# A post-norm decoder block: four products in column quarters, the bias product added to the residual, the last group's squares summed by products, and new places for every step

## The chip, the cores and the metric

The kernel runs on one core of a Trainium2 chip. TensorE (PE in the profile, PEld for its weight loads) multiplies, VectorE (DVE) and ScalarE (ACT) empty PSUM and do element work, GpSimd (POOL) does element work in SBUF alone, and SyncE (SP) issues nearly all DMAs. The metric is the device time of one execution in microseconds (us); less is better.

## What is computed

x is 128 sequences of 64 tokens by 128 features, and there is a context of the same shape. One decoder layer with a layer norm (LN) after each of its three parts:

```python
q, k, v = x@Wq+bq, x@Wk+bk, x@Wv+bv                  # 16 heads of 64
qp, kp = exp(q @ wq_feat), exp(k @ wk_feat)          # 32 features a head
x1 = LN(x + concat(qp @ (kp.T @ v) / (qp @ kp.sum(tokens) + 1e-6)) @ Wproj + bproj)
Q, K, V = x1@cWq.T+cbq, ctx@cWk.T+cbk, ctx@cWv.T+cbv # 16 heads of 8
x2 = LN(x1 + concat(softmax(Q @ K.T / sqrt(8)) @ V) @ Wo.T + bo)
h  = layernorm(gelu(x2 @ tern(W_fc).T), ln_w, ln_b)  # 512 hidden
out = LN(x2 + h @ tern(W_proj).T)
```

`tern` turns a weight into -1, 0 or 1. All of it is float32. The kernel folds weights together first: Wq and wq_feat, Wv and Wproj (the tile U), the biases (WB), the inner layer norm's weight and mean (w2c).

## The kernel before

The 8192 token rows are cut into 16 groups of 512 (8 sequences). For each group, `load`, `attn`, `cross` and `ffn` define short steps, each with a name: K0 to K3 and Q0 to Q3 are the feature products, ks and kT sum the keys, G is kp.T by x, D and dT make the denominators, E multiplies qp by their inverse, M is G by U, Y is qp by M and the residual, Yn the norm. Then xk, xq and xv make the cross attention's K, Q and V, X the scores for the row maxima, xm sends the maxima, S the scores again with exp, P the product with V, C the normalization, O the output product, xn the norm. ft, fb, fw, fs, fo, fv, fx and fn are the feed-forward part and the last norm; fn also stores the group.

Nothing is scheduled by the compiler. Each step has a place, `g * ROUND + SHIFT + PLACE` (ROUND is 44; a step of the weights' preparation has its place in PREP), and the program is the list of steps sorted by place (line 929). All engines take their instructions in that order. A group's steps spread over more than three rounds, so each round of the steady state holds attention of group g, cross attention of g-1 and g, and feed-forward of g-2 and g-3; cross and ffn steps are keyed by r = g + 1. Loads stand a round early.

PSUM has two pools: `one`, four tiles of 128x512, and `two`, two tiles of 128x1024. A step that asks for a tile waits until an earlier tile of that pool was read for the last time. fo0 and fo1 keep a `one` tile each until fx has read it.

A product of float32 is two MATMUL and two LDWEIGHTS instructions in the trace; one of fp32r operands (K, Q, E, fw, xk, xq, G) is one of each. A product is issued in one of several forms: with all 128x128 of the array (`128*128` in the trace), in four column quarters (`128*32`: four products, each with 32 columns of weights and 32 PSUM partitions, tile_position (0, 32j); M, Y, D, P and ks do this), or in row halves or 64x64 pieces (G, X, S).

Lines that the change touches: 596 is M's product, 610 Y's first product (dT by WB) and 615 its other products, 617 the sum with the residual xg; 635 the six copies of a product's pieces into krep or qrep by DMA, 659 xv's product, 712 the four DMAs of the row maxima, 771 O's product, 816 fs's square on ACT, 819 and 822 the sums of squares on POOL (line 410 in the trace), 833 fo's product and 834 the product that sums the squares over the hidden units.

```python
ps = z.fps[k] = one()
for i in range(2):
    n = slice((2 * k + i) * P, (2 * k + i) * P + P)
    o = 256 * i
    for c in range(NFC):
        nc.tensor.matmul(ps[:, o : o + WF], lhsT=z.gf[c // 2][:, c % 2, n], rhs=w.w2c[:, c, :], start=(c == 0), stop=(c == NFC - 1))
    nc.tensor.matmul(ps[:, o + WF : o + WF + 1], lhsT=z.sq[:, n], rhs=rff, start=True, stop=True)
```

Of the kernel before, what the change touches and what calls it, by code (L numbers as in the profile page):

```python
# [55 lines left out]
)  # L56
BIG = 5
# [27 lines left out]
def decoder_block(  # L85
# [347 lines left out]
    def shift(g, place):  # L433
        return SHIFT[2 if place[0] == "f" else 1 if place[0] in "xXSPCO" else 0].get(g, 0)
# [47 lines left out]
    def attn(g):  # L482
# [118 lines left out]

        @each(g, [f"Y{t}" for t in range(GT)])
        def _(t):
            if t == 0:
                z.x1 = later.l2.tile([P, GT, D], FP, tag="x1", name="x1")
                z.mv1 = st.tile([P, GT, 2], FP, tag="mv1", name="mv1")
            yps = one()
            for i in range(4):
                n = slice(t * P + 32 * i, t * P + 32 * i + 32)
                nc.tensor.matmul(yps[32 * i : 32 * i + 32, 0:D], lhsT=z.dT[:, n].bitcast(FP), rhs=w.WB.bitcast(FP), start=True,  # L610
                                 stop=False, tile_position=(0, 32 * i))
            for c in range(NC1):
                for i in range(4):
                    q = 2 * t + i // 2
                    nc.tensor.matmul(yps[32 * i : 32 * i + 32, 0:D], lhsT=z.qp[:, c, t * P + 32 * i : t * P + 32 * i + 32],  # L615
                                     rhs=z.m[q // 4][:, q % 4, c, :], start=False, stop=(c == NC1 - 1), tile_position=(0, 32 * i))
            nc.vector.tensor_tensor(z.x1[:, t, :], yps[:, 0:D], z.xg[:, t, :], ALU.add)
            stats(z.mv1, t, z.x1[:, t, :])
            if t == GT - 1:
                z.rs1 = rstd_of(z.mv1)  # L620
# [5 lines left out]
    def pieces(step, ps, bias, roles, rep):  # L626

        pc = later.t2.tile([P, 3, GN], BF, tag="pc", name="pc")
        nc.scalar.activation(pc[:, 0, :], ps, AF.Identity, bias=bias)
        r = later.t2.tile([P, GN], FP, tag="tmp", name="pr")  # L630
        nc.vector.scalar_tensor_tensor(r, ps, bias, pc[:, 0, :], ALU.add, ALU.subtract)
        copy(f"{step}1", pc[:, 1, :], r)
        tt(f"{step}2", pc[:, 2, :], r, pc[:, 1, :], ALU.subtract)
        for i, part in enumerate(roles):
            nc.sync.dma_start(out=rep[i::HD], in_=pc[:, part, :])

    def cross(g):
# [18 lines left out]
        def _():  # L656
            ps = one()
            for t in range(GT):
                nc.tensor.matmul(ps[:, t * P : t * P + P], lhsT=z.cT[:, t * P : t * P + P],
                                 rhs=w.cwvT.rearrange("p o c h e -> p (o c h e)"), start=True, stop=True)  # L660
# [42 lines left out]
        def _():  # L703
# [5 lines left out]
            for i in range(2):  # L709
                for h in range(2):  # L710
                    o = 64 * h + R2 - 2 + i
                    nc.sync.dma_start(out=qrep[o : o + 1], in_=mn[32 * h : 32 * h + 32, i, :])
# [52 lines left out]
        def _(k):  # L765
# [4 lines left out]
            for i in range(2):  # L770
                nc.tensor.matmul(ps[:, i * D : i * D + D], lhsT=z.cnT[k][:, i, :], rhs=w.cwo, start=True, stop=True)
# [11 lines left out]
    def ffn(g):  # L783
# [30 lines left out]
        def _(k):  # L814
            s = later.f1.tile([P, 2, GN], FP, tag="sk", name="sk")
            nc.scalar.activation(s.rearrange("p i n -> p (i n)"), z.gf[k].rearrange("p i n -> p (i n)"), AF.Square)  # L816
            if k == 0:
# [8 lines left out]
        @each(r, ("fo0", "fo1"))  # L826
        def _(k):
            ps = z.fps[k] = one()
            for i in range(2):
                n = slice((2 * k + i) * P, (2 * k + i) * P + P)  # L830
                o = 256 * i
                for c in range(NFC):
                    nc.tensor.matmul(ps[:, o : o + WF], lhsT=z.gf[c // 2][:, c % 2, n], rhs=w.w2c[:, c, :], start=(c == 0), stop=(c == NFC - 1))  # L833
                nc.tensor.matmul(ps[:, o + WF : o + WF + 1], lhsT=z.sq[:, n], rhs=rff, start=True, stop=True)  # L834
# [87 lines left out]
    groups = [SimpleNamespace(pt={}, kp={}, khl={}, cps={}, cnT={}, mps={}, gT={}, m={}, gf={}, fps={}) for _ in range(NG)]  # L922
# [52 lines left out]
```

## Time and profile before

| | |
|---|---|
| time, median of 3 runs | 740.73 us (740.13 to 741.4) |
| the profiled execution | 740.87 us, its span 738.9 us |
| mean granted TensorE clock | 0.966 |
| busy | PE 687.4, PEld 576.9, DVE 572.9, ACT 504.3, POOL 323.4 us |
| one steady round (374.68 to 415.36) | 40.68 us; PE 40.31, DVE 34.99, ACT 31.31, POOL 18.79 us busy |
| first 60 us | PE 49.4 us busy |
| from 660 us to the end (78.9 us) | PE 47.9 us busy |
| instruction DMA, queue q8 | 129 packets, 2.11 MB |

The span is from the first to the last instruction. A row of the timeline has the start in us, the length in us, the engine, the line, the operation, the tile written and the tiles read, the shape and the count of merged instructions; in brackets stands the idle time before it and what ended it. The lengths of matmuls overlap, so the cost of a product is read from the start of one row to the start of the next. In a row of the windows stand the stretch, its length, each engine's busy time, the granted clock of TensorE (1.00 is full), and the DMA engines' share and rate.

### The profile page before, as it was taken

The numbers are of one execution on the slowest core, as the hardware profiler recorded it, in microseconds if no ns is written. First come the engines' busy times: TensorE is split into PE (matmuls) and PEld (weight loads), VectorE is DVE, ScalarE is ACT, GpSimd is POOL, SyncE is SP. The second block draws the span as 40 slices with busy tenths as digits, with TensorE's granted clock in tenths as the row PEclk, the third lists the DMA queues.
The fourth block names the chain that finished last, engine by engine and source line by source line (L and its number), as shares of the span: only waits on it lengthen the run. The fifth ranks groups of instructions, "written<-read, shape, count | busy, mean of one in ns | idle before, by whom it ended". The sixth has DMA issues, their size and how long they took to land.

```text
span 738.9 us, 36655 instructions
## 1 busy us (share of the span) xinstructions
PE 687.4 (93%) x16551; PEld 576.9 (78%) x16551; DVE 572.9 (78%) x1379; ACT 504.3 (68%) x757; POOL 323.4 (44%) x383
## 2 busy tenths in 40 slices
PE   6989999999999999999999999999999999976753
PEld 5767878787878888887878788887888787865653
DVE  1568898797879797988879787979889796958532
ACT  2636565867688687877686886878686877654750
POOL 4744414263553626263634526262635445143451
PEclk9989999999999999999999999999999999996875
DMA  7005131302122131413032221314131312203000
GB/s 191 3 31 136 43 106 31 102 24 77 55 75 75 49 101 34 117 34 92 31 84 65 76 75 47 103 34 116 35 80 42 82 53 52 71 24 82 19 23 20
DMA packets 58428, 47.82 MB, mean 65 GB/s; under 512 B 7952, under 2 KB 54032, under 8 KB 58272
## 3 DMA queue, kind: packets, MB, share of 16 engines
q1 hardware_dynamic: 57632, 45.37, 22.6%
q8 instruction: 129, 2.11, 1.2%
q0 software_dynamic: 320, 0.08, 0.2%
q14 instruction: 27, 0.22, 0.1%
q10 hardware_dynamic: 320, 0.03, 0.0%
HBM read 15.58 MB, written 4.19 MB: 27 GB/s over the span
## 4 chain that ended last, share of the span: by engine, by line
PE 68%; DVE 18%; POOL 4%; ACT 4%; DMA 2%; issue 2%; SPq 1%; POOLq 0%; ACTq 0%; DVEq 0%
PE two L596 13%; PE one L833 8%; PE one L615 8%; PE one L427 6%; PE one L428 4%; PE one L429 4%; PE two L530 3%; DVE bns L390 3%; PE two L697 3%; POOL rstd L385 2%; PE one L517 2%; DVE x L851 2%; PE one L610 2%; DVE gT L395 2%; PE one L582 2%
## 5 line engine op out<-in xcount | busy, mean ns | idle before, releaser
L596 PE MATMUL two<-U,gT 128*32 128x128 f32 x4096 | 123.4, 275 | 0.8 <-DVE mx L700 0.5
L596 PEld LDWEIGHTS two<-U,gT 128*32 128x32 f32 x4096 | 112.0, 111 | 1.8 <-DVE mx L700 0.6
L397 ACT COPY m<-two 128x1024 f32<-128x1024 f32 x64 | 64.9, 1013 | 30.3 <-PE two L596 30.1
L399 POOL TENSOR_SCALAR khl<-kp 128x512 fp32r<-128x512 f32 x32 | 20.2, 631 | 137.6 <-ACT kp L496 137.6
L833 PE MATMUL one<-w2c,gf 128*128 128x130 f32 x512 | 78.1, 301 | 1.5 <-ACT gf L810 1.5
L700 DVE TENSOR_REDUCE mx<-two 128x16 f32<-128x1024 f32 x64 | 74.9, 1213 | 3.3 <-PE two L697 3.3
L833 PEld LDWEIGHTS one<-w2c,gf 128*128 128x128 f32 x512 | 71.4, 210 | 4.8 <-ACT gf L810 2.1
L410 POOL TENSOR_TENSOR sq<-sk 128x512 f32<-128x512 f32 x16 | 20.8, 1299 | 116.9 <-ACT sk L816 116.9
L385 POOL TENSOR_TENSOR rstd<-veps,mhalf 128x4 f32<-128x4 f32 x64 | 66.0, 1032 | 5.3
L615 PE MATMUL one<-m,qp 128*32 128x128 f32 x2048 | 68.1, 273 | 0.0
L383 POOL TENSOR_SCALAR veps<-mv 128x4 f32<-128x4 f32 x64 | 15.4, 240 | 116.2 <-DVE mv L844 73.8
L423 ACT ACTIVATE x<-x,nm,rstd 128x128 f32<-128x128 f32 x128 | 51.3, 482 | 20.6 <-DVE nm L422 20.6
L728 ACT ACTIVATE pt<-two 128x1024 f32<-128x1024 f32 x64 | 62.7, 1021 | 1.9 <-PE two L725 1.7
L390 DVE BATCH_NORM_STATS2 bns<-x 128x6 f32<-128x128 f32 x192 | 55.5, 289 | 5.5
L615 PEld LDWEIGHTS one<-m,qp 128*32 128x32 f32 x2048 | 57.4, 110 | 0.2 <-issue 0.2
L508 ACT ACTIVATE qp<-one,bqk 128x512 f32<-128x512 f32 x64 | 43.7, 684 | 16.3 <-PE one L429 12.0
L496 ACT ACTIVATE kp<-one 128x512 f32<-128x512 f32 x64 | 38.3, 598 | 22.0 <-PE one L429 13.5
L530 PE MATMUL two<-khl,xgh 64*128 64x512 f32 x256 | 49.0, 418 | 4.6 <-DVE gT L395 4.3
L707 ACT ACTIVATE mn<-one 64x128 bf16<-64x128 f32 x16 | 4.3, 270 | 70.1 <-PE one L705 70.1
L744 PE MATMUL one<-pt,vbd 128*32 128x64 f32 x2048 | 46.7, 224 | 0.5 <-DVE x L851 0.5
L410 POOL TENSOR_TENSOR sq<-sq,sk 128x512 f32<-128x512 f32 x32 | 40.9, 1280 | 6.1 <-ACT sk L816 4.8
L842 DVE COPY mv<-one 128x2 f32<-128x2 f32 x32 | 4.9, 154 | 49.4 <-PE one L834 49.4
(217 smaller groups left out, 1812.6 us busy)
## 6 DMA issues: line engine op xcount, KB each, us to landing
krep<-pc SPq DMA_DIRECT2D x96, 128.0 KB, 2.4
qrep<-pc SPq DMA_DIRECT2D x96, 128.0 KB, 3.0
xT<-in_x_T_dram SPq DMA_DIRECT2D x16, 256.0 KB, 3.1
xg<-in_x_dram SPq DMA_DIRECT2D x16, 256.0 KB, 3.1
cT<-in_ctx_T_dram SPq DMA_DIRECT2D x16, 256.0 KB, 3.3
out_dram<-x SPq DMA_DIRECT2D x16, 256.0 KB, 2.4
qrep<-mn SPq DMA_DIRECT2D x64, 8.0 KB, 1.8
wTk<-in_L_attn_Wk_T_dram SPq DMA_DIRECT2D x1, 512.0 KB, 4.4
```

Source lines behind the costliest of these rows:

```text
L385: nc.gpsimd.tensor_tensor(r, v, mhalf, ALU.pow)
L390: nc.vector.bn_stats(s, src)
L397: nc.scalar.copy(dst, src)
L410: eng.tensor_tensor(dst, a, b, op)
L423: nc.scalar.activation(x[:, t, :], x[:, t, :], AF.Identity, scale=r[:, t : t + 1], bias=nm[:, t : t + 1])
L530: nc.tensor.matmul(gps[:, b, :], lhsT=xp[r, t, :], rhs=z.khl[t // 2][r, kp, t % 2, :], start=(i == 0), stop=(i == 2), tile_position=(64 * ...
L596: nc.tensor.matmul(z.mps[b // 2][32 * j : 32 * j + 32, b % 2, c * D : c * D + D], lhsT=z.gT[b // 4][:, b % 4, h * F : h * F + F], rhs=w.U[ ...
L615: nc.tensor.matmul(yps[32 * i : 32 * i + 32, 0:D], lhsT=z.qp[:, c, t * P + 32 * i : t * P + 32 * i + 32], rhs=z.m[q // 4][:, q % 4, c, :], ...
L700: nc.vector.tensor_reduce(z.mx[:, :, :, t], sps.rearrange("p h (c k) -> p h c k", k=S), AX.X, ALU.max)
L728: nc.scalar.activation(z.pt[t].rearrange("p h b c q -> p (h b c q)"), sps.rearrange("p h n -> p (h n)"), AF.Exp, scale=HD ** -0.5)
L744: nc.tensor.matmul(z.cps[i // 4][32 * c : 32 * c + 32].rearrange("p (n k q) -> p n k q", k=2, q=32)[:, q // 32 : q // 32 + 2, k, :], lhsT= ...
L833: nc.tensor.matmul(ps[:, o : o + WF], lhsT=z.gf[c // 2][:, c % 2, n], rhs=w.w2c[:, c, :], start=(c == 0), stop=(c == NFC - 1))
```

## The change

The same sums are computed, in other forms and another order.

1. Products in column quarters: xv, O, and fo with its sum of squares. Each product with 128 columns of weights becomes four with 32.
2. A new step W makes dT by WB for the whole group, four full fp32r products, and adds it to xg; Y's own quarter products for this are gone (before, they read the same fp32r tiles as float32).
3. In the last group the POOL sums of squares are gone: fo multiplies the four squared tiles themselves with the column 1/512, accumulating in PSUM, and the second square has a buffer of its own.
4. `pieces` issues its six DMAs sorted by part, not by row; xm's four DMAs of 32x128 become two of 64x128.
5. All places are new, and EDGE adds a further shift to single steps of groups -1, 0, 1, 14, 15 and 16.

```diff
 def shift(g, place):
-    return SHIFT[2 if place[0] == "f" else 1 if place[0] in "xXSPCO" else 0].get(g, 0)
+    return SHIFT[2 if place[0] == "f" else 1 if place[0] in "xXSPCO" else 0].get(g, 0) + EDGE.get(g, {}).get(place, 0)
...
+        @at(g, "W")
+        def _():
+            ps = one()
+            for t in range(GT):
+                n = slice(t * P, t * P + P)
+                nc.tensor.matmul(ps[:, n], lhsT=z.dT[:, n], rhs=w.WB, start=True, stop=True)
+            nc.vector.tensor_tensor(z.xg.rearrange("p t d -> p (t d)"), ps, z.xg.rearrange("p t d -> p (t d)"), ALU.add)
...
-            for i in range(4):
-                n = slice(t * P + 32 * i, t * P + 32 * i + 32)
-                nc.tensor.matmul(yps[32 * i : 32 * i + 32, 0:D], lhsT=z.dT[:, n].bitcast(FP), rhs=w.WB.bitcast(FP), start=True,
-                                 stop=False, tile_position=(0, 32 * i))
...
-        for i, part in enumerate(roles):
+        for part, i in sorted((part, i) for i, part in enumerate(roles)):
             nc.sync.dma_start(out=rep[i::HD], in_=pc[:, part, :])
...
             for t in range(GT):
-                nc.tensor.matmul(ps[:, t * P : t * P + P], lhsT=z.cT[:, t * P : t * P + P],
-                                 rhs=w.cwvT.rearrange("p o c h e -> p (o c h e)"), start=True, stop=True)
+                for j in range(4):
+                    r = slice(32 * j, 32 * j + 32)
+                    nc.tensor.matmul(ps[r, t * P : t * P + P], lhsT=z.cT[:, t * P : t * P + P][:, r],
+                                     rhs=w.cwvT.rearrange("p o c h e -> p (o c h e)"), start=True, stop=True,
+                                     tile_position=(0, 32 * j))
...
             for i in range(2):
-                for h in range(2):
-                    o = 64 * h + R2 - 2 + i
-                    nc.sync.dma_start(out=qrep[o : o + 1], in_=mn[32 * h : 32 * h + 32, i, :])
+                nc.sync.dma_start(out=qrep[R2 - 2 + i :: R2], in_=mn[:, i, :])
...
-            s = later.f1.tile([P, 2, GN], FP, tag="sk", name="sk")
+            s = later.f1.tile([P, 2, GN], FP, tag="sk1" if k and g == NG - 1 else "sk", name="sk")
             nc.scalar.activation(s.rearrange("p i n -> p (i n)"), z.gf[k].rearrange("p i n -> p (i n)"), AF.Square)
-            if k == 0:
+            if g == NG - 1:
+                z.sk[k] = s
+            elif k == 0:
...
                 for c in range(NFC):
-                    nc.tensor.matmul(ps[:, o : o + WF], lhsT=z.gf[c // 2][:, c % 2, n], rhs=w.w2c[:, c, :], start=(c == 0), stop=(c == NFC - 1))
-                nc.tensor.matmul(ps[:, o + WF : o + WF + 1], lhsT=z.sq[:, n], rhs=rff, start=True, stop=True)
+                    for j in range(4):
+                        q = slice(32 * j, 32 * j + 32)
+                        nc.tensor.matmul(ps[q, o : o + WF], lhsT=z.gf[c // 2][:, c % 2, n][:, q], rhs=w.w2c[:, c, :],
+                                         start=(c == 0), stop=(c == NFC - 1), tile_position=(0, 32 * j))
+                for j in range(4):
+                    q = slice(32 * j, 32 * j + 32)
+                    sq = [z.sk[c // 2][:, c % 2, n] for c in range(NFC)] if g == NG - 1 else [z.sq[:, n]]
+                    for c, s in enumerate(sq):
+                        nc.tensor.matmul(ps[q, o + WF : o + WF + 1], lhsT=s[:, q], rhs=rff, start=(c == 0),
+                                         stop=(c == len(sq) - 1), tile_position=(0, 32 * j))
```

O is changed as xv is. The new places are a table; sorted by them, a steady round (the seventh, counted from 0 the sixth) reads as follows, with g left out:

```
before: P0 P1 S2 P2 P3 S3 fx xk G0 G1 D0 D1 P4 D3 P6 C0 xt G2 G3 K0 xq fw0 D2 M0 dT P5 M1 P7 fs0 M4 M5 M2 M3 C1 fw1 O0
        K1 E2 E1 xv X0 X1 K2 lc lx E0 ks0 xs ks1 M6 M7 E3 K3 lgs O1 X2 X3 fs1 Y0 ks2 Y2 Y1 ks3 Y3 xm Q0 Q1 fn xn fo0 Q3 lg
        kT xr S0 S1 Q2 Yn fo1 fv ft lxs fb
after:  xs Q0 ft Q2 S0 S1 fo1 Q3 Q1 Yn S3 lg fb fv P0 P1 P2 P3 fx S2 xk G0 G1 D0 lxs D2 D1 D3 P4 C0 xt G2 G3 dT xq fw0
        P6 M0 P5 P7 M1 M4 M5 E2 E1 fw1 C1 xr E3 E0 K0 K1 M2 M3 O0 fs0 lx ks0 xv X0 X1 W K2 K3 lc X2 ks1 ks2 Y0 M6 fs1 X3 O1
        lgs M7 Y2 xm fn xn ks3 Y1 fo0 Y3 kT
```

In the last rounds the order is looser. After the last group's Y3 before come 15.xm, 13.fo0, 15.S0, 15.S1, 15.Yn, 13.fo1, 13.fv, 14.ft, and only after 15.P0 to 15.S3 16.xk, 13.fx, 16.xt, 16.xq; after the change come 15.S0, 13.fo1, 13.fv, 13.fx, 15.S2, 15.Yn, 15.P0, 15.P1, 15.S1, 15.S3, 16.xk, 14.ft, 16.xt, 16.xq. (The number is the round's key: 16.xq is the last group's.) At the very end 15.fo1 moves ahead of 16.xn, 15.fo0 between 16.ft and 16.fw0, and 15.fx behind 16.fo0. In the first round the fill of krep and qrep (x2) moves from behind M5 of group 0 to behind its ks1, the bias tiles (wb) from behind D3 to behind Q0, and x is loaded straight after the key weights. The store of group 0 (its fn) moves into the round of group 14.

More of the change, by code (lines that the diff above doesn't have):

```diff
@@ L47 @@
 SHIFT = (
[8 rows of a table removed]
-)
[6 rows of a table added]
+)
+EDGE = {
[7 rows of a table added]
+        "lgs": 3.841, "lx": 47.153, "lxs": 21.118},
[40 rows of a table added]
+}
 BIG = 5
@@ L615, in _ @@
                     nc.tensor.matmul(yps[32 * i : 32 * i + 32, 0:D], lhsT=z.qp[:, c, t * P + 32 * i : t * P + 32 * i + 32],
-                                     rhs=z.m[q // 4][:, q % 4, c, :], start=False, stop=(c == NC1 - 1), tile_position=(0, 32 * i))
+                                     rhs=z.m[q // 4][:, q % 4, c, :], start=(c == 0), stop=(c == NC1 - 1), tile_position=(0, 32 * i))
             nc.vector.tensor_tensor(z.x1[:, t, :], yps[:, 0:D], z.xg[:, t, :], ALU.add)
@@ L770, in _ @@
             for i in range(2):
-                nc.tensor.matmul(ps[:, i * D : i * D + D], lhsT=z.cnT[k][:, i, :], rhs=w.cwo, start=True, stop=True)
+                for j in range(4):
+                    r = slice(32 * j, 32 * j + 32)
+                    nc.tensor.matmul(ps[r, i * D : i * D + D], lhsT=z.cnT[k][:, i, r], rhs=w.cwo, start=True, stop=True,
+                                     tile_position=(0, 32 * j))
             nc.vector.tensor_tensor(z.x2[:, 2 * k : 2 * k + 2, :], ps[:, 0 : 2 * D].rearrange("p (i e) -> p i e", i=2),
@@ L832, in _ @@
                 for c in range(NFC):
-                    nc.tensor.matmul(ps[:, o : o + WF], lhsT=z.gf[c // 2][:, c % 2, n], rhs=w.w2c[:, c, :], start=(c == 0), stop=(c == NFC - 1))
-                nc.tensor.matmul(ps[:, o + WF : o + WF + 1], lhsT=z.sq[:, n], rhs=rff, start=True, stop=True)
+                    for j in range(4):
+                        q = slice(32 * j, 32 * j + 32)
+                        nc.tensor.matmul(ps[q, o : o + WF], lhsT=z.gf[c // 2][:, c % 2, n][:, q], rhs=w.w2c[:, c, :],
+                                         start=(c == 0), stop=(c == NFC - 1), tile_position=(0, 32 * j))
+                for j in range(4):
+                    q = slice(32 * j, 32 * j + 32)
[3 more added lines that the diff above has]
+                                         stop=(c == len(sq) - 1), tile_position=(0, 32 * j))
         @at(r, "fv")
@@ L920, in _ @@
                                 ALU.subtract)
-    groups = [SimpleNamespace(pt={}, kp={}, khl={}, cps={}, cnT={}, mps={}, gT={}, m={}, gf={}, fps={}) for _ in range(NG)]
+    groups = [SimpleNamespace(pt={}, kp={}, khl={}, cps={}, cnT={}, mps={}, gT={}, m={}, gf={}, sk={}, fps={}) for _ in range(NG)]
     for g in range(NG):
```

94 rows, old and new, of tables (EDGE, PLACE, PREP, SHIFT) are left out of this document.

## The prediction

> **What bounds the kernel now.** I read the busy shares and slices, then the windows, the timeline of TensorE in one round, and last the chain at the end. From the page:
>
> ```profile
> PE 687.4 (93%) x16551; PEld 576.9 (78%) x16551; DVE 572.9 (78%) x1379; ACT 504.3 (68%) x757; POOL 323.4 (44%) x383
> PEclk9989999999999999999999999999999999996875
> ```
>
> PE is busy 93% and its clock is below nine tenths only in the third slice and the last four. The windows of one round and of the end:
>
> ```profile
> 374.68:415.36 40.68, 40.31 (x1035) 34.22 (x1027) 34.99 (x83) 31.31 (x48) 18.79 (x21) 1.00 0.25 69
> 660.00:680.00 20.00, 12.97 (x323) 9.56 (x315) 14.38 (x34) 11.57 (x16) 8.54 (x9) 0.80 0.31 81
> 700.00:720.00 20.00, 12.02 (x64) 10.41 (x64) 8.99 (x34) 9.88 (x18) 11.30 (x12) 0.76 0.05 15
> ```
>
> A steady round is PE's (40.31 of 40.68 us); only fewer or denser PE instructions shorten it. The end is a chain with PE 60 to 65% busy at a lowered clock.
>
> How dense each form is, start to start:
>
> ```profile
> 371.39 1.06 PE L833 MATMUL one<-w2c,gf 128*128 128x130 f32 x8
> 372.29 0.28 PE L834 MATMUL one<-rff,sq 128*128 128x1 f32 x2
> 372.43 1.14 PE L833 MATMUL one<-w2c,gf 128*128 128x130 f32 x8
> 373.40 0.28 PE L834 MATMUL one<-rff,sq 128*128 128x1 f32 x2
> 373.55 0.63 PE L792 MATMUL one<-ident,x 128*128 128x128 f32 x4
> ...
> 379.21 0.41 PE L556 MATMUL one<-qp,kblk 128*32 128x64 f32 x16
> 379.44 0.41 PE L744 MATMUL one<-pt,vbd 128*32 128x64 f32 x16
> 379.77 0.66 PE L670 MATMUL one<-ident,x 128*128 128x128 f32 x4
> ...
> 402.46 0.40 PE L610 MATMUL one<-WB,dT 128*32 128x128 f32 x8
> 402.68 1.06 PE L615 MATMUL one<-m,qp 128*32 128x128 f32 x32
> 403.55 0.40 PE L610 MATMUL one<-WB,dT 128*32 128x128 f32 x8
> ```
>
> A quarter instruction takes 27.3 ns at 128 columns (0.87/32) and 14 ns at 64 (0.23/16); a full one takes 0.90/8 = 112 ns, as much as four quarters. So quarters save little by themselves. Before a change of form the next product starts late (0.33 instead of 0.23 for 16), so a **switch** costs 0.10 us. The second product behind a switch into the full form is late by 0.10 more (in K0 after G3, 382.40, 382.73, 382.96: 0.33, then 0.23).
>
> **The change in a steady round.** (a) fo: its two halves take 372.43 - 371.39 = 1.04 and 373.55 - 372.43 = 1.12 us. After: 32 quarters of 130 columns, 32 x 27.3 x 130/128 = 0.89, and 8 of one column, whose price no row shows. Nearest is 14 ns (64 columns): 0.11. Together 1.00 a half: -0.16 a step, **-0.32** a round. Bounds: 10 ns, the 64 pieces of X from 394.84 to 395.48 in 0.64 us, and 27.3 ns, as if columns did not matter: -0.44 to +0.12.
>
> The Trainium skill, "TensorE: Matmul & The Clock Gate", section "Wait — 56ns, not 53.3ns?", speaks against this: a matmul never starts less than about 25 ns after the last, however few columns it has; the rows at 10 and 14 ns contradict it, and by it the eight would take 0.20, a round 0.36 us more than I reckon.
>
> (b) W: Y loses 32 quarters, 4 x 0.22 = 0.87 us. Four full fp32r products of 128 columns come. The trace has fp32r only at 512 columns (0.23 us), full products of 128 at 0.112: 0.45 us if fp32r keeps one pass, 0.87 if it needs float32's two instructions' time. I take 0.45, the row nearest in form: **-0.42** (up to 0). W stands between X1 and K2, so it adds no full stretch. Its sum on DVE is one 128x512 operation, 0.69 us as x2l (line 796); DVE goes from 34.99 to 35.7 us of a 40 us round. Queued behind it are X2's maximum and Y0's sum; PE meanwhile has K2, K3 and ks. Without that cover X3's PSUM turn is 0.7 late.
> (c) xv: 8 full at 0.112 = 0.89 become 32 x 27.3 = 0.87; O the same in halves: 0.
> (d) Switches, counted in the two listed orders: 22, of them 8 into full, become 24, 7 into full: +0.20 - 0.10 = **+0.10**.
> Sum: -0.64 a round, bounds -0.8 to +0.2. Eight undisturbed rounds (groups 4 to 12): **-5 us** (-6 to +2). The rounds of 13 and 14 count 28 and 34 switches for 22 and 26, and 4 more entries: **+2**.
>
> DMAs: `pieces` issues the same six, xm two for four, on SP, which no step waits for in a round but through qrep, covered by Yn and Q. Group 0's fn (ACT 1.6 us, one 256 KB store) moves past some 13 rounds of SP's queue into ACT's slack of 9 us a round; its x2 keeps one of six buffers, and a group needs its own for 2.3 rounds. Instruction DMA grows by 4,700 on 33,100 PE instructions, 14%: q8 used 1.2% of the engines. Free.
>
> **The start.** E of group 0 waits at 42.1 and again at 44.5:
>
> ```profile
> 36.83 3.52 POOL L371 MEMSET qrep<- 128x4096 bf16 x1
> 36.94 3.48 DVE L571 CAST di<-rd 128x128 fp32r<-128x128 f32 x1
> 42.09 0.50 PE L582 MATMUL one<-dT,E 128*128 128x512 f32 x1 [1.43 <-DVE last L369]
> 42.13 2.29 DVE L370 CAST krep<-last 128x4096 bf16<-128x4096 f32 x1
> 44.54 0.80 PE L582 MATMUL one<-dT,E 128*128 128x512 f32 x1 [1.26 <-DVE nhalf L325]
> ```
>
> A cast that takes 0.23 in a round took 3.48 beside POOL's fill; then krep's fill held DVE, and PE fell to half clock until 51. With the fills ahead of Q2 these 1.4 + 1.3 and some 3 us of half clock go; late next is POOL (wb, 5 us, ahead of the splits of K1 and K3). Against it: fbd's memsets behind c0 (DVE 1.1 us) start the first product as much later, and some 20 more switches. Net **-3** (-8 to +4).
>
> **The end.** The last group's Y3 ends at 649.8, its xq at 668.8. Between, PE waited 1.9 us for qrep<-mn, xt 1.7 for PSUM (held by fo until fx), and x1l stood on DVE behind 13.fx (3.1 us). After: fo1 (2.1) and fv (1.1) end 3.5 us after Y3, rstd (1.3) 4.9, fx 8, Yn (2.1) 10.1, xk's pr and x2l 11.6, x1l 12.8, xq 13.6 instead of 19.0: -5.4. `pieces` issues one DMA behind its last part, not four (0.6 each): -1.5; xm two, not four: -1. But C and O of 15 (6.5 us of DVE) now stand before X's maxima: +2. xn no longer stands behind 14.fn (1.6 us of ACT), but fo0 stands before fw0: -0.5. Last, fo:
>
> ```profile
> 714.30 0.71 PE L833 MATMUL one<-w2c,gf 128*128 128x130 f32 x4 [1.29 <-ACT gf L810]
> 717.43 2.60 POOL L410 TENSOR_TENSOR sq<-sq,sk 128x512 f32<-128x512 f32 x2 [1.17 <-ACT sk L816]
> 720.08 0.59 PE L834 MATMUL one<-rff,sq 128*128 128x1 f32 x2 [5.07 <-POOL sq L410]
> 720.53 2.08 PE L833 MATMUL one<-w2c,gf 128*128 128x130 f32 x8
> ```
>
> PE waited 5.07 us for three POOL sums and then ran at half rate (8 in 1.87, not 0.90) until 726.8. After, the second square needs only its gf (715.3), and PE runs on from 714.3: four halves of 0.89 + 32 x 14 ns = 5.3 us at full clock. Half clock lasts some 4 us after an idle stretch (701.6 to 705.8), so 5.3 + 2.1 = 7.4: 721.7. **-5**. Sum of the end -11 (-18 to -3, since orders of four engines are traded).
>
> **Sum.** -5 + 2 - 3 - 11 = -17: the span goes from 738.9 to 722; with the 2.0 us around it (740.87 - 738.9), **724 us**. The profiled execution is 0.14 above the median; no correction.
>
> **Rivals.** (1) *More at both ends* (15%): the start gives 8 and the end 17: 713. For: PE is idle for 31 of the last 79 us. Against: every trade must succeed.
> (2) *DVE takes the rounds back* (15%): only xq, fw0, three P and four M stand between dT and E2; before there were five M, fw1, O0 and K1. From D3 to E2 PE has 8.6 us, DVE C0 (2.0), x1l (0.7), gT (1.2) and dT's operations (4.0), in a round that W fills further. If E waits 0.8 us a round, eight rounds cost 6: 730. Against: all of E's idle time before, 2.7 us, is the two waits of group 0.
> (3) *The change doesn't do what it says* (13%): W at 0.87 (+0.42) and one-column quarters at 27 ns (+0.44) leave +0.2 a round: 724 + 8 x 0.86 = 731.
> (4) *Slower: PSUM turns* (12%). From fo0 to fx two of the four `one` tiles are held. Before, four other tiles (Q3, Q2, ft, P0) pass through the rest; after, seven (Y3, Q0, ft, Q2, Q3, Q1, P0). Q's tile is free only when ACT's exp (0.69) is done, behind S's exps (1.0 each). Three such turns missed cost 3 x 0.69 = 2.1 us a round, 12 rounds 25: 749. It decides from 1.4 us a round on (17/12). For: PEld waited 0.41 for kT's PSUM before fo at 367.6. Against: PE's waits for ACT sum to 3 us in the whole trace.
>
> **Numbers.** Forecast case 45%, within 716 to 731. The range, 711 to 737, leaves out (4) and the far end of (1). Within 0.2% (739.3 to 742.2, about what a measurement of this kernel can tell from no change) lie only edges: 3%, two taken from (2) and (3), one from (4). Faster: 45 + 15 + 15 + 13 - 2 = 86%; slower: 12 - 1 = 11%.
>
> **What would show it.** Rounds of 40.0 us between starts of xk (0.1 up or down tells (a), (b) and (d) apart: half of fo 1.00, W 0.45); E of group 0 before 40 us; no POOL sum in the last group, its xq 14 us after Y3, fo done by 722. Wrong if rounds stay at 40.7 with PE waiting for DVE (2) or ACT (4), or if the last Y3 comes no earlier.

## The result, and the profile after

The changed kernel takes 752.06 us (median of 4 runs, 749.91 to 754.76); the kernel before 740.76 beside it. The ratio is 1.0154, 95% interval 1.0117 to 1.0191: slower, where 724 us were forecast. The profiled execution took 753.11 us, its span 751.2.

From the page (busy times, the instruction queue with its packets and MB), then the windows of one round and of the two stretches of the end:

```profile
PE 686.0 (91%) x18887; PEld 552.9 (74%) x18887; DVE 586.1 (78%) x1395; ACT 504.2 (67%) x757; POOL 323.3 (43%) x380
q8 instruction: 148, 2.42, 1.3%
```

```profile
262.46:303.50 41.04, 39.94 (x1177) 32.77 (x1167) 35.48 (x85) 31.27 (x48) 18.98 (x20) 1.00 0.26 69
660.00:680.00 20.00, 17.21 (x698) 14.55 (x687) 15.56 (x47) 12.21 (x21) 6.37 (x8) 1.00 0.08 19
700.00:720.00 20.00, 16.53 (x503) 12.49 (x493) 11.16 (x40) 14.67 (x20) 8.44 (x9) 0.84 0.02 5
```

PE is busy for less time than before and yet the span is longer: in a round it now stands still for 1.1 us (41.04 - 39.94) where it stood for 0.37. The end is denser than before, but it begins later. The forms themselves came out cheaper than forecast, as the timeline of PE at fo shows:

```profile
298.11 1.10 PE L896 MATMUL one<-w2c,gf 128*32 128x130 f32 x32
299.02 0.22 PE L902 MATMUL one<-rff,sq 128*32 128x1 f32 x8
299.08 1.08 PE L896 MATMUL one<-w2c,gf 128*32 128x130 f32 x32
```

32 quarters take 0.91 us, and eight one-column quarters 0.06 (7 ns each): a half of fo is 0.97, where 1.00 was forecast.

Where the time went, by stretches of PE's timeline (xk of round 4 starts at 171.9 and 178.8, xk of round 13 at 539.2 and 556.7, the last Y ends at 649.8 and 672.6):

| stretch | before | after | difference | forecast |
|---|---|---|---|---|
| start to xk of round 4 | 171.9 | 178.8 | +6.9 | -3 |
| nine rounds to xk of round 13 | 367.3 | 377.9 | +10.6 | -5 |
| to the end of the last Y | 110.6 | 115.9 | +5.3 | +2 |
| to the end | 89.1 | 78.6 | -10.5 | -11 |
| span | 738.9 | 751.2 | +12.3 | -17 |

In the nine rounds the view of PE's waits (total, times, longest) had G's wait for gT as its largest row before (the first row here); after the change its two largest rows are of things that had no row there before:

```profile
PE two L530 <- DVE gT L395: 3.3, 9, 0.4
...
PE one L478 <- DVE x1l L732: 9.2, 9, 1.1
PE one L896 <- issue: 2.8, 3, 1.4
```

The second product of xq waits for x1l in every one of these rounds, and fo stands still without waiting for anything ("issue"). All gaps of the second kind, reckoned from PE's starts as what exceeds the spacing that each form has elsewhere, are 0.3 us in the nine rounds before and 6.4 after. (The same reckoning is used below; it also counts what is too short for the view of waits.)

Why x1l is late stands in the timeline of all engines in one such round:

```profile
308.17 0.59 ACT L447 CAST x1h<-one 128x512 fp32r<-128x512 f32 x1
...
308.34 1.29 POOL L460 TENSOR_TENSOR xTl<-xT,xTh 128x512 fp32r<-128x512 f32 x1 [0.23 <-ACT xTh L447]
308.35 1.56 DVE L460 TENSOR_TENSOR cn<-cd,rs 128x256 f32<-128x256 f32 x1
...
310.31 0.65 DVE L732 TENSOR_TENSOR x1l<-one,x1h 128x512 fp32r<-128x512 f32 x1
...
311.02 0.50 PE L478 MATMUL one<-x1l,cwqh 128*128 128x512 f32 x1 [1.10 <-DVE x1l L732]
```

x1h is there at 308.76. DVE could make x1l at about 309.2, but its operation cn, in C0, takes 1.56 us. It began 10 ns behind POOL's xTl, the lower half of the next group's input, and ended 0.28 us after it. In the kernel before, cn takes 0.42 every time; here it runs while POOL is idle, and DVE's row is the same otherwise:

```profile
300.16 0.42 DVE L410 TENSOR_TENSOR cn<-cd,rs 128x256 f32<-128x256 f32 x1
300.62 0.45 DVE L762 STREAM_TRANSPOSE cnT<-cn 128x256 f32<-128x256 f32 x1
300.99 0.65 DVE L674 TENSOR_TENSOR x1l<-one,x1h 128x512 fp32r<-128x512 f32 x1
```

The change moved the step that makes xTl, lxs, from place -1.03 to 16.30, shortly ahead of C0 and xt. So the theory is **contention**: a DVE operation that reads and writes SBUF stands still while POOL works there. The rivals: DVE simply has too much between fx and x1l (**chain**), or the new forms starve PE of instructions and the rest follows (**forms**).

### The profile page after: what moved, and what is told of

It reads as the page before. It is cut to its first block, busy times and chain, and to the rows that moved or that the text cites. A ratio compares the mean times of both kernels' runs of the same rounds, so it can differ in the third digit from the quotient of the medians.

```text
span 751.2 us, 41431 instructions
## 1 busy us (share of the span) xinstructions
PE 686.0 (91%) x18887; PEld 552.9 (74%) x18887; DVE 586.1 (78%) x1395; ACT 504.2 (67%) x757; POOL 323.3 (43%) x380
## 4 chain that ended last, share of the span: by engine, by line
PE 55%; DVE 22%; POOL 8%; issue 7%; ACT 6%; DMA 2%; ACTq 0%; SPq 0%; POOLq 0%; DVEq 0%
PE two L646 13%; PE one L670 5%; PE one L896 5%; PE one L477 4%; POOL rstd L435 4%; PE one L478 3%; PE one L479 3%; DVE bns L440 3%; DVE cn L460 2%; DVE gT L445 2%; PE one L632 2%; POOL sq L460 2%; PE one L800 2%; PE two L755 2%; DVE x L920 2%
## 5 line engine op out<-in xcount | busy, mean ns | idle before, releaser
L646 PE MATMUL two<-U,gT 128*32 128x128 f32 x4096 | 127.8, 273 | 0.3
L758 DVE TENSOR_REDUCE mx<-two 128x16 f32<-128x1024 f32 x64 | 76.5, 1217 | 3.5 <-PE two L755 3.1
L896 PE MATMUL one<-w2c,gf 128*32 128x130 f32 x2048 | 72.5, 287 | 3.4 <-issue 2.8
L896 PEld LDWEIGHTS one<-w2c,gf 128*32 128x32 f32 x2048 | 58.2, 115 | 6.9 <-issue 4.5
L670 PEld LDWEIGHTS one<-m,qp 128*32 128x32 f32 x2048 | 55.8, 110 | 3.0 <-issue 1.2
L633 DVE TENSOR_TENSOR qp<-qp,one 128x512 f32<-128x512 f32 x64 | 40.8, 674 | 6.5 <-PE one L632 6.5
L800 PE MATMUL one<-pt,vbd 128*32 128x64 f32 x2048 | 41.2, 221 | 1.9 <-ACT pt L784 1.1
L460 POOL TENSOR_TENSOR khl<-kp,khl 128x512 fp32r<-128x512 f32 x32 | 41.3, 1291 | 2.7
L445 DVE COPY gT<-two 128x1024 f32<-128x1024 f32 x32 | 38.8, 1213 | 3.2 <-PE one L670 1.9
L800 PEld LDWEIGHTS one<-pt,vbd 128*32 128x32 f32 x2048 | 32.9, 110 | 11.1 <-issue 8.2
```

Source lines behind the costliest of these rows:

```text
L445: nc.vector.tensor_copy(dst, src)
L460: eng.tensor_tensor(dst, a, b, op)
L646: nc.tensor.matmul(z.mps[b // 2][32 * j : 32 * j + 32, b % 2, c * D : c * D + D], lhsT=z.gT[b // 4][:, b % 4, h * F : h * F + F], rhs=w.U[ ...
L758: nc.vector.tensor_reduce(z.mx[:, :, :, t], sps.rearrange("p h (c k) -> p h c k", k=S), AX.X, ALU.max)
L800: nc.tensor.matmul(z.cps[i // 4][32 * c : 32 * c + 32].rearrange("p (n k q) -> p n k q", k=2, q=32)[:, q // 32 : q // 32 + 2, k, :], lhsT= ...
L896: nc.tensor.matmul(ps[q, o : o + WF], lhsT=z.gf[c // 2][:, c % 2, n][:, q], rhs=w.w2c[:, c, :], start=(c == 0), stop=(c == NFC - 1), tile_ ...
```

## The experiments

Ratios are to the kernel before, run beside each on the same chip, with 95% intervals; its medians there were between 738.7 and 742.6 us, so ratios are compared, and times only roughly. The changed kernel stands at 1.0154.

### Forms and order apart

First, all of the new code in the order of before:

```diff
-PREP, SHIFT, PLACE, EDGE of the changed kernel
+PREP, SHIFT, PLACE of before; EDGE = {}; "W": 26.9700
```

> All of the new forms (quarters, W, squares by products, sorted pieces) in the order of before (its three tables, no EDGE; W directly behind E3). Theory order: the loss comes from the new order (start +7, x1l late on DVE 11 us), so the forms alone gain their 0.3 to 0.6 us in each of some 13 rounds and up to 5 us at the last squares: 729 to 736. Theory forms: the 14% more PE instructions starve TensorE of instructions (gaps without a wait, 6.9 us in nine rounds of the changed kernel) wherever they stand: 739 to 744. Rival W: its sum on DVE delays X2 and Y; rounds then show PE waits of 0.7 us behind W, and the time is 738 or more.

Measured: 746.07 us, 1.0090 (1.0056 to 1.0125). And the other way round, the code of before with the tables of the changed kernel:

> The code of before with the three tables and EDGE of the changed kernel. Theory order: the wait of xq for x1l (11 us in the trace) and the late start (+7) stay, and the last squares are summed on POOL again: 750 to 758. Theory forms: without the added instructions the gaps go and the new order is as good as the old or better: 735 to 745.

Measured: 775.98 us, 1.0475 (1.0441 to 1.0508). Both times lie outside both theories' ranges: the two theories asked the wrong question. Each half alone is slower than the kernel before, and the changed kernel is faster than the new order with the old forms by 24 us, so forms and order cannot be priced apart. Waits of 0.7 us behind W, as the first expectation's rival asks, the trace does not have. PE's changes of form per round, counted in the traces: before 22.0 (8.0 into the full form), changed 24.3 (7.2), new forms in the old order 29.0 (10.3), old forms in the new order 28.9 (10.9). By the prediction's prices of 0.10 and 0.10, seven more changes and 2.3 more entries cost 0.93 us a round, about what fo (0.4 by the lengths above) and W (0.4) save. In the second kernel x1l is late as well (11.7 us by PE's starts in nine rounds, 10.6 by the same count in the changed kernel): so that wait belongs to the order, and the gaps without a wait belong to the forms (5.9 us with the new forms in the old order, 0.9 with the old forms in the new).

### C0 behind xt

```diff
-"C0": 61.6682,
+"C0": 62.4000,
```

> The changed kernel with one place moved: C0 of a round behind xt, so that DVE does x1l before C0's four operations (2.0 to 3.2 us). PE's order is untouched. Theory order: xq's second product no longer waits for DVE, 1.0 us in 11 rounds come back: 740 to 743. Rival: the wait only moves (to gT, dT or to the PSUM tile that C0 frees later): 749 to 753.

Measured: 759.55 us, 1.0260 (1.0227 to 1.0293). The rival held, and worse: x1l now waits 1.47 us for x1h at the head of DVE's queue, C0 and the second gT stand behind it, and M waits 6.7 us for gT in seven of the nine rounds. A wait cannot be cured by passing the same late work to the next in the queue.

### fo in the full form

```diff
-nc.tensor.matmul(ps[q, o : o + WF], lhsT=z.gf[c // 2][:, c % 2, n][:, q], rhs=w.w2c[:, c, :],
-                 start=(c == 0), stop=(c == NFC - 1), tile_position=(0, 32 * j))
+nc.tensor.matmul(ps[:, o : o + WF], lhsT=z.gf[c // 2][:, c % 2, n], rhs=w.w2c[:, c, :], start=(c == 0), stop=(c == NFC - 1))
...
-nc.tensor.matmul(ps[q, o + WF : o + WF + 1], lhsT=s[:, q], rhs=rff, start=(c == 0),
-                 stop=(c == len(sq) - 1), tile_position=(0, 32 * j))
+nc.tensor.matmul(ps[:, o + WF : o + WF + 1], lhsT=s, rhs=rff, start=(c == 0), stop=(c == len(sq) - 1))
```

> The changed kernel with fo (products and one-column sums) in the full form of before; the last group keeps its squares by products. 120 fewer PE instructions a round. Theory forms: the gaps without a wait (6.9 us in nine rounds, most of them within fo) fall below 1 us, while fo itself costs 0.1 us more a half and two switches into full form: 747 to 750. Theory order: the gaps are small change, and the time rises by fo's own 0.2 to 0.4 us in 16 rounds: 753 to 758.

Measured: 760.07 us, 1.0259 (1.0220 to 1.0297), above both ranges; the profiled execution, 755.93, is the fastest. Its gaps without a wait fell from 6.4 to 1.4 us, as the theory of forms said; but PE's work without gaps and waits rose by 0.53 us a round (0.18 of it changes of form, at those prices), and the rounds are as long as with quarters (42.05 and 41.99). In the trace, then, the quarters are worth about what their instructions' gaps cost. Why the other executions are up to 7 us slower, no trace shows.

### lxs behind xt

```diff
-"lxs": 16.2973,
+"lxs": 17.3000,
```

> The changed kernel with one place moved, lxs (ACT's copy xTh, POOL's difference xTl of the next group) from ahead of xt to behind it. In the changed kernel POOL's xTl begins 10 to 40 ns before DVE's cn, and cn takes 1.56 us in the eleven rounds in which xq's second product waits 1.2 us for x1l, against 0.42 in the rounds without it. Theory contention (a DVE operation from SBUF to SBUF stands still while a POOL operation runs): cn takes 0.42 again, the wait goes, 11 x 1.2 = 13 us: 737 to 741. Rival chain (DVE simply has too much between fx and x1l): x1l comes at most 0.4 earlier, and gT or dT is late in its place: 748 to 752. Rival order of ACT: the 0.6 us for which x1h now comes ahead of xTh is all that is won, 6 us: 746.

Measured: 741.04 us, 0.9993 (0.9974 to 1.0012): 1.6% or 12 us of the 13 expected. The timeline of the same place:

```profile
303.61 0.42 DVE L460 TENSOR_TENSOR cn<-cd,rs 128x256 f32<-128x256 f32 x1
...
304.39 1.29 POOL L460 TENSOR_TENSOR xTl<-xT,xTh 128x512 fp32r<-128x512 f32 x1 [1.02 <-ACT xTh L447]
304.44 0.65 DVE L732 TENSOR_TENSOR x1l<-one,x1h 128x512 fp32r<-128x512 f32 x1
...
305.14 0.50 PE L478 MATMUL one<-x1l,cwqh 128*128 128x512 f32 x1
```

POOL's xTl is as long as ever, but beside it now stands x1l, which reads PSUM and keeps its 0.65 us. cn has its 0.42 again, and PE's lateness is 0.1 to 0.2. Contention holds. Chain falls, since DVE has the same operations between fx and xq, and so does the order of ACT, whose 0.6 us explain no more than 746. But the nine rounds take 366.8 us now, where the kernel before took 367.3: with the wait gone, the gaps still use up what PE's own work saves.

### The same neighbours in the kernel before, and without POOL

The kernel before with one place changed:

```diff
-"lxs": -1.0251,
+"lxs": 7.4500,
```

> The kernel before with one place moved: lxs from -1.03 to 7.45, directly ahead of C0 and xt, where the changed kernel has it. Everything else is the kernel before. Theory contention: cn goes from 0.42 to 1.5 us, xq's second product waits about 1.2 us for x1l in eleven to thirteen rounds: 752 to 757. Rival (the wait belongs to the changed kernel's whole order): cn stays at 0.42 or its delay is covered, 740 to 744.

Measured: 756.91 us, 1.0245 (1.0216 to 1.0275). One place costs 18 us. Here too, in the timeline, POOL is 10 ns ahead and xq comes late:

```profile
308.83 1.29 POOL L410 TENSOR_TENSOR xTl<-xT,xTh 128x512 fp32r<-128x512 f32 x1 [0.23 <-ACT xTh L397]
308.84 1.56 DVE L410 TENSOR_TENSOR cn<-cd,rs 128x256 f32<-128x256 f32 x1
...
311.51 0.50 PE L427 MATMUL one<-x1h,cwqh 128*128 128x512 f32 x1 [0.83 <-DVE x1l L674]
```

cn takes 1.55 to 1.56 in twelve rounds, and K's product waits for xTl besides (0.16 a round). The changed kernel with its order as it is, but xTl made by DVE:

```diff
-"lx": "G",
+"lx": "V",
```

> The changed kernel with its order as it is, but the difference xTl computed on DVE (0.69 us) instead of POOL (1.29), so that no POOL operation stands beside cn. Theory contention: cn takes 0.42 again; with xTl's 0.69 in front of it x1l comes 0.45 earlier, 5 us over eleven rounds: 745 to 748. Rival chain (DVE has too much between fx and x1l, POOL has no part in it): x1l comes 0.7 later and the wait grows: 757 to 762.

Measured: 778.39 us, 1.0527 (1.0494 to 1.0561), outside both. The edit did not take POOL away from this place, it brought the next POOL operation forward, and that met xTl itself:

```profile
316.57 1.29 POOL L460 TENSOR_TENSOR xb<-x,bo_bc 128x512 f32<-128x512 f32 x1
...
316.78 1.62 DVE L460 TENSOR_TENSOR xTl<-xT,xTh 128x512 fp32r<-128x512 f32 x1 [0.98 <-ACT xTh L447]
...
319.45 0.42 DVE L460 TENSOR_TENSOR cn<-cd,rs 128x256 f32<-128x256 f32 x1
```

cn is short again, and xTl takes 1.62 us instead of the 0.69 that DVE needs for such an operation elsewhere; it also waits for ACT's xTh ahead of all of C0 and x1l. That the same kind of stretching moves to whatever stands beside POOL speaks for contention; the time itself does not separate the theories. Part of it is another thing: between 140 and 600 us the granted clock falls to half in eight stretches, 31 us in all, where the changed kernel has full clock throughout.

### The start

```diff
-"c0": -216.2333,
+"c0": -205.0000,
```

> The changed kernel with one place of the preparation moved: the constants c0 behind lk, as in the kernel before, so that DVE clears fbd first and its DMAs are issued at 1.0 instead of 2.2 us. Theory start: the first product comes at 6.3 instead of 10.2 us and all that follows is 4 us earlier: 747 to 749. Rival: the first product is early but the products then wait for wTk, x's loads or the later fills, which stand as they do: 751 to 753.

Measured: 749.80 us, 1.0126 (1.0098 to 1.0153), between the two ranges: 2 us less than the changed kernel, with overlapping intervals. In the trace the first product comes at 6.13 instead of 10.16 and xk of round 4 4.4 us earlier. Both edits together:

> Both of the moves above together. If each removes its own wait, their gains add: 733 to 737, faster than the kernel before. If the rounds' own speed hides the start or the other way round: no better than the better of the two.

Measured: 734.33 us, 0.9906 (0.9871 to 0.9941): 2.5% less than the changed kernel, where the two moves alone gave 1.6 and 0.3, so the gains at least add, and this kernel is faster than the one before. By the stretches of the table it is 3.4 us behind that one at xk of round 4, loses 0.2 in the nine rounds and 3.8 up to the last Y, and gains 10.4 behind it: what is faster is the end, not the rounds. Its start is no shorter in the trace than with lxs alone (xk of round 4 at 175.3 and 175.6), for it holds another collision (timeline of all engines):

```profile
26.56 1.89 POOL L367 TENSOR_TENSOR bsel<-bsel,bv 128x1024 f32<-128x1024 f32 x1
26.78 5.21 DVE L396 COPY cwvT<-cwv 128x128 f32<-128x128 f32 x1
...
28.40 3.51 POOL L421 MEMSET qrep<- 128x4096 bf16 x1
...
32.06 0.48 PE L405 MATMUL one<-ident,wo 128*128 128x128 f32 x1 [4.76 <-DVE wo L403]
```

DVE's copy cwvT ends when POOL's product and fill are over, 5.21 us for an operation of 0.23. It began 0.22 us behind the product; in the trace with c0 alone moved it began 0.19 us ahead of it (25.79 and 25.98) and took 0.22. With the fills moved ahead, to a time when both engines wait for weights:

```diff
-"x2": 16.5468,
+"x2": -70.0000,
```

> The kernel with lxs behind xt and c0 behind lk, and one more place: x2 (DVE's fill of krep, POOL's fill of qrep) at -70 instead of 16.5, ahead of the first K, while both engines wait for weights. In the trace without this move DVE's copies cwvT and wo take 5.2 and 3.5 us beside POOL's fill (28.4 to 31.9) and TensorE waits 4.8 + 1.9 us for them. Theory contention: both waits go, all from the first round on is 4 to 6 us earlier: 728 to 731. Rival: POOL's other long runs (16 memsets, 4.3 us, and a product of 1.9 us) hold DVE as long, so that the wait stays: 733 to 735.

```profile
28.95 0.23 DVE L396 COPY cwvT<-cwv 128x128 f32<-128x128 f32 x1
...
30.05 0.33 PE L405 MATMUL one<-ident,wo 128*128 128x128 f32 x1 [0.58 <-DVE wo L403]
```

Measured: 733.38 us, 0.9871 (0.9841 to 0.9902), the lowest ratio of all. The time lies in the rival's range, but the rival's condition did not occur: PE's wait for wo fell from 4.76 to 0.58 us. In the trace the first xk comes 5.4 us earlier (56.7 for 62.1), also because the half clock from 29.0 to 39.3 us of the trace without the move does not occur; by the ratios about 2.6 us of it arrive, with overlapping intervals. The profiled execution ran at a granted clock of 0.95 from 23 us on where the others had 1.00, so its later rounds cannot be compared.

### W, the last squares, xv and O, the stores

Four single parts, the last a test of the gaps, each against the kernel with lxs and c0 moved (0.9906), xv and O against the one with lxs alone (0.9993):

```diff
-@at(g, "W")
...
+nc.tensor.matmul(yps[32 * i : 32 * i + 32, 0:D], lhsT=z.dT[:, n].bitcast(FP), rhs=w.WB.bitcast(FP), start=True,
+                 stop=False, tile_position=(0, 32 * i))
```

> The kernel with lxs behind xt and c0 behind lk, without W: the bias product again as 32 quarter instructions within Y. By the trace W's four products take 0.4 to 0.5 us and the quarters 0.9, so W is worth 0.4 us in each of 16 rounds: 740 to 742 without it. Rival: W's sum on DVE costs as much as the products save: 733 to 736.

Measured: 743.69 us, 1.0005 (0.9980 to 1.0029). W is worth 1.0% or 7.3 us (3 more or less), 0.46 a round; the nine rounds of the traces give 0.42 (371.3 us for 367.5).

```diff
-if g == NG - 1:
-    z.sk[k] = s
-elif k == 0:
+if k == 0:
...
-sq = [z.sk[c // 2][:, c % 2, n] for c in range(NFC)] if g == NG - 1 else [z.sq[:, n]]
+sq = [z.sq[:, n]]
```

> The kernel with lxs behind xt and c0 behind lk, but with the squares of the last group summed on POOL as in all other groups. The prediction gave this edit 5 us of the end: 739 to 741. Rival: in the new order the sums are hidden in part behind the gelu and the square on ACT: 735 to 738.

Measured: 736.08 us, 0.9916 (0.9893 to 0.9939): not to be told from the kernel with them, and in the rival's range. In its timeline PE again waits for POOL's sum, and the last fo takes 11.9 us from its first product to its last; with the squares by products it takes 9.6:

```profile
716.84 0.29 PE L900 MATMUL one<-rff,sq 128*32 128x1 f32 x8 [5.40 <-POOL sq L460]
```

```diff
-nc.tensor.matmul(ps[r, i * D : i * D + D], lhsT=z.cnT[k][:, i, r], rhs=w.cwo, start=True, stop=True, tile_position=(0, 32 * j))
+nc.tensor.matmul(ps[:, i * D : i * D + D], lhsT=z.cnT[k][:, i, :], rhs=w.cwo, start=True, stop=True)
```

> The kernel with lxs behind xt, and xv and O in the full form of before: 48 PE instructions fewer in each of 16 rounds, the products themselves as long (0.89 for 0.87 us). Theory fetch: a third of the added instructions goes and so does a third or more of the 6 us of gaps without a wait: 2 to 3 us less than with lxs alone. Rival form: the entries into the full form (0.2 us each, three a round) cost more than that: 4 to 9 us more than with lxs alone.

Measured: 743.75 us, 1.0030 (1.0004 to 1.0056), 2.7 us (2.3 more or less) more than with quarters, between the two ranges. That the entries into the full form weigh more than the 48 instructions fits, but is not shown: the only trace is of an execution of 1689.29 us, more than twice the others, in which nothing can be compared.

```diff
-nc.sync.dma_start(out=of[g], in_=z.x2)
+if g < 2 or g > 12: nc.sync.dma_start(out=of[g], in_=z.x2)
```

> The kernel with lxs behind xt and c0 behind lk, which leaves out the output's stores of groups 2 to 12 (11 x 256 KB), so that their rows stay unwritten. Some of the gaps without a wait stand right behind such a store. Theory collision (the instructions' DMA waits behind the store's packets): the gaps, 6.5 us in nine rounds, fall by half or more: 729 to 732. Theory density (a stretch of short instructions is used up faster than its blocks come): they stay above 5 us: 733 to 735.

Measured: 737.71 us, 0.9909 (0.9872 to 0.9947), and the gaps without a wait are 7.4 us in the nine rounds, not fewer. Collision with the stores falls; density stands, though by its rival's fall and not by a test of its own.

### Group 14's own places

```diff
-    14: {"C0": 2.399, "C1": 1.125, "D0": 2.127, "D1": 3.571, "D2": 4.857, "D3": 2.645, "E0": 7.899, "E1": 3.613,
...
+    14: {"fb": 28.437, "fn": 130.955, "fo0": 50.242, "fo1": 45.386,
...
```

> The kernel with lxs behind xt, c0 behind lk and the fills early, without the 14th group's own places but for its feed-forward steps and loads. Reckoned from the traces, the stretch from the start of round 13 to the last Y takes 4 to 5 us longer than in the kernel before, and the stretch behind that Y 10 us less. If group 14's own order is what costs the 4 to 5 us and brings nothing: 729 to 731. If it is what prepares the short end: 736 to 742.

Measured: 736.53 us, 0.9962 (0.9944 to 0.9979), against 0.9871 with them. Round 13 is 3 us shorter (40.0 for 43.0) and round 14 4.5 longer (48.5 for 44.0). So these places do not cost the 5 us between round 13 and the last Y: without them that stretch takes 118.2 us for 115.0, and the end behind the last Y 79.8 for 78.5 (the second number of each at the granted clock of 0.95). What those 5 us are made of is left open; part is the x1l wait of round 13 and the gaps.

## Why the prediction was wrong, step by step

**(a) fo, (b) W, (c) xv and O: right.** A half of fo is 0.97 for the 1.00 forecast, with a one-column quarter at 7 ns, below the lower bound of 10. W undone costs 0.46 us a round for the 0.42 forecast. The rule of at least 25 ns from one product to the next, which the prediction quotes from the Trainium skill ("TensorE: Matmul & The Clock Gate", section "Wait — 56ns, not 53.3ns?"), has the eight one-column quarters at 0.20 us; they take 0.06, four quarters in turn.

**(d) The changes of form: counted rightly** (24 and 7; the trace has 24.3 and 7.2). The runs showed how much hangs on them: in the wrong order the same forms are slower than none.

**The sum of a round, -0.64: failed**, above all because of two terms that it did not have. PE's own work fell by 0.32 us a round (361.8 to 358.9 us in nine rounds without gaps and waits), half of what the terms give. By the same starts the changed products save 0.79 (fo 0.38, W 0.36, xv and O 0.05), and products whose form did not change take some 0.4 more, 0.17 of it Y's; the sum had only (d)'s 0.10 for them, and why they take more I cannot say. On top came 1.0 us of x1l's wait and 0.7 us of gaps, and 0.2 of small waits, less 0.4 that G no longer waits for gT: +1.2 by the sum of the stretch. The shortest rounds of the kernels without x1l's wait take 39.5 to 40.3 us, about the forecast's 40.0, but their mean with lxs moved is 40.75, as before (40.81).

**"Its sum on DVE ... PE meanwhile has K2, K3 and ks": right for W, but it was the wrong operation to ask about.** The durations of DVE's row were taken over from the order of before. The prediction itself quoted the row that forbids it, a cast of 3.48 us for 0.23 beside POOL's fill, used it for one place of the start, and never asked which DVE operation stands beside which POOL operation in the new order. The listed order after the change has lxs shortly ahead of C0. This is the step that failed first: x1l was taken to be ready in time, and cn's 1.56 us for 0.42 made xq wait 1.0 us a round.

**"Instruction DMA ... Free": failed.** The queue's share is indeed 1.3%, but a share says nothing of lateness. The gaps without a wait grew from 0.3 to 6.4 us in nine rounds, 0.7 us a round where the sum had nothing.

**The start, -3: failed, +6.9.** c0 ahead of lk was priced at DVE's 1.1 us; the first product came 3.8 later (10.16 for 6.32), and c0's place alone brought that back (6.13). That fbd's small DMAs, issued 1.2 us later, fell in behind larger loads is likely, but not shown. And the fills, which no longer met E's cast, met cwvT instead (4.51 us in this kernel): the collision was moved, not removed. The half clock was moved as well, 6.8 us from 43.9 before and 6.8 us from 33.9 after, and E of group 0 comes at 46.9, not before 40.

**The end, -11: right in sum**, -10.5, and in its largest part. From the last Y to xq's first product it is 11.6 us instead of 17.0 (-5.4, as forecast). The last squares gave about 2.3 of their 5 us within PE's timeline (9.6 for 11.9 us, in the kernels with lxs and c0 moved) and too little to be told by the ratios: PE waits 0.66 us more for ACT's second square and runs 3.4 us at half clock. Also their products were priced at 14 ns. At full clock they take about 22, as the changed kernel's last half shows (32 starts from 738.42 to 739.09):

```profile
738.42 0.85 PE L902 MATMUL one<-rff,sk 128*32 128x1 f32 x32
```

Here four squares of one quarter follow each other, where fo changes the quarter with every product. That the sum came out nearly right although this term was twice too large is luck; which other term made up for it, no run shows.

**The rivals.** (2), DVE takes the rounds back, is the nearest: right that DVE would, at 1.0 us a round instead of 0.8, but at xq's second product and not at E, and for another reason than a full queue. (4) landed near the time (749) by a mechanism that did not occur: PE's waits for PSUM turns behind ACT stay under 0.2 us a round.

## What to carry to other kernels

When an order is changed, a duration taken from the old trace holds only beside its old neighbours: list for each moved POOL operation the DVE operations that it will now meet, and price those that were seen to stand still beside such an operation at POOL's end. Count changes of form for a set of forms and an order together, for a form that saves in one order loses in another. And look at the idle time that waits for nothing before calling more instructions free.

## What the runs showed of the hardware

**DVE and POOL.** Eleven times in the changed kernel and twelve times in the kernel before with one place moved, cn (two inputs in SBUF) starts 8 to 17 ns behind POOL's xTl (1.29 us), takes 1.55 to 1.57 us and ends 0.28 after it; alone it takes 0.42. A copy in SBUF takes 4.5 and 5.2 us beside POOL's product and fill, and 0.23 without. Operations that read PSUM (x1l, gT) keep their length beside POOL. The delay depends on what is left of POOL's operation: in the sixteen traces that can be read, cn begins 102 times while a 128x512 operation of POOL has more than 0.2 us to run, and ends 0.28 to 0.29 us after it each time, taking 0.57 to 1.57. The Trainium skill, "SBUF — State Buffer", section "SBUF: two separate sides", says that DVE and GpSimd share a pair of ports under an exclusive lock, which a DVE operation in a two-port mode takes, and one with two SBUF inputs only against a GpSimd operation that reads SBUF; whichever starts first keeps it for its whole instruction and the other stands still. The rows agree: cn stands for as long as xTl runs, and is done soon after. Not every POOL operation has this effect:

```profile
338.68 1.04 POOL L435 TENSOR_TENSOR rstd<-veps,mhalf 128x4 f32<-128x4 f32 x1
338.72 0.71 DVE L460 TENSOR_TENSOR cTl<-cT,cTh 128x512 fp32r<-128x512 f32 x1
```

POOL's rstd, of 128x4, reads SBUF and runs 1.04 us, and beside it cTl, with two inputs in SBUF, keeps its length (0.69 to 0.71 in 146 cases, 0.68 alone), as does cn (0.42 in 17 cases).

**Instructions.** Here is such a gap in the timeline of PE, within fo:

```profile
340.06 0.86 PE L896 MATMUL one<-w2c,gf 128*32 128x130 f32 x20
342.30 0.43 PE L896 MATMUL one<-w2c,gf 128*32 128x130 f32 x8 [1.38 <-issue]
```

I set the ends of all such gaps of more than 0.25 us, between 100 and 600 us, beside the packets of the instruction queue in seven traces: 63 of 64 gaps end 1.2 to 1.6 us after a packet has landed (this one landed at 340.88). A packet lands every 4.5 us or so there, so chance would put about one gap in eleven into that window; no run changes the fetch itself. The packets are 16 KB, one for about 255 instructions of PE and PEld (2 x 18887 / 148). Over nine rounds the gaps are 0.0 to 0.9 us in the three kernels with 16,551 PE instructions, 1.4 with 16,895, and 4.5 to 7.4 with 18,791 to 19,335 (the kernel with xTl on DVE, whose rounds run in part at half clock, is left out). The Trainium skill, "Runtime: NRT & Kernel Launch", section "Instruction fetch mechanics", has the same blocks, of 16 KiB or 256 instructions, but calls the fetch hidden because instructions are issued more slowly than they come in; here, in quarters at 28 ns and one-column quarters at 7 ns, the rows speak against that.
